# A two-layer graph kernel: the order of its opening, its scratch space, and layer 1's norms on another engine

## The chip, the cores and the metric

One core of one Trainium2 chip runs the whole program. Its engines work side by side, each through its own queue in order: TensorE (PE in the profile, with its weight loads as PEld), VectorE (DVE), ScalarE (ACT), GpSimd (POOL), and SyncE (SP), which only issues DMAs. ScalarE and GpSimd issue DMAs too. The metric is device time in microseconds; a comparison takes the median of several runs. Beside these runs one execution is recorded by the hardware profiler, and all readings of the trace are of that one.

## What is computed

The input is `x`, 2708 nodes by 256 features, and a weighted adjacency matrix `adj` of 2708 by 2708. Two layers follow each other, each inside a residual and a layer norm without weights:

```python
# layer 0: two steps of walk and attention
R = (adj + I) / row sums
for n in range(2):
    A  = top-p attention of Xa          # softmax of q k^T, smallest set of mass 0.9, normalised
    Xf = R @ Xf
    Xa = A @ Xa
    Z  = Z + Xf @ U1[n].T + Xa @ U2[n].T
h = layernorm(X + Z) * ln_g + ln_b
x = layernorm(x + h)
# layer 1: graph attention, 4 heads of 64
Wh = x @ W                              # per head
e  = leaky_relu(s_i + s_j)              # masked by adj != 0 or the diagonal
h' = softmax_j(e) @ Wh
out = layernorm(x + h')
```

So each row passes two norms at the end of layer 0 and one at the end of layer 1. ln_g and ln_b are loaded and applied as inputs.

## The kernel before, in words

Rows are cut into 22 tiles, sixteen of 128 rows and six of 110 (`rows`, `off`); `groups` are up to four tiles of the same height. Everything is float32. The loops are unrolled, and a scheduler orders the instructions of each engine, except inside `tc.manual_schedule`, where TensorE, VectorE, ScalarE and GpSimd keep the order in which the code is written. SP's queue is always ordered by the scheduler, so a load can be pulled far ahead if its buffer is free. Tiles of closed pools give their space to later pools; a new tile waits until what lay there before has been read.

**Opening** (L533 to L1072, outside the manual order). ScalarE's queue issues g_sb and b_sb (L116, L117), then the attention weights w1, w2, w3 (L539 to L542) and u_sb (L547); SP's issues x (`load_x`). Two small products make the query weights (L592 to L599). Then for each group of tiles x is transposed on TensorE (L1063), copied out by ScalarE and VectorE (L1068, L1069), and projected to q and k (`project`, L613), whose halves VectorE and ScalarE copy (L617, L618).

**Layer 0** is driven by `slot`: each call moves the searches for the top-p threshold (`going`, mostly VectorE), the rows under way (`doing`) and a stream of walk products (`walks`, L878) one step on. `walks` loads the adjacency in half columns (`blk`, pool `adjp` of 3 buffers), one block ahead. `step` runs the attention of 22 rows (`turned`, `weigh`, L225 to L243). `finish` ends a row: it adds up the terms, and for rows 0 to 17 goes through `norms` (norm, times ln_g, plus x and ln_b, norm) and `sources` (transpose, product with the layer-1 weights, exponentials, four scaled copies, store of the values to DRAM as `vd`). The four last rows are late: their sums stay in `xe` and their norms and sources run in layer 1.

**A norm** (`layernorm`, L131 to L139) is three VectorE instructions for mean and variance, a power on GpSimd for 1/sqrt, and after a `yield` one VectorE instruction that subtracts and multiplies. A `yield` gives way until the next call, so what stands behind it comes later in every queue.

**Layer 1** (`layer1`) goes through three groups of target rows (8, 8 and 6 tiles: 1024, 1024 and 660 columns), and for each through all 22 source tiles in pairs. A source tile needs its adjacency block, made 0 or 1 by ScalarE (`neighbours`, Sign and Square, L1187 and L1188), four weight tiles by VectorE (`weights`, L1258), and sixteen values and denominators products on TensorE (`values` L1269, `denominators` L1279). Masks are made three tiles ahead (`mask`), weights two. `beside` is called twice a pair and moves other work one step on: in group 0 the late rows (`prepared`) and the check of the shortcuts (`verdict`), two of them at a time (`late[:2]`); in groups 1 and 2 the rows of the group before (`settle`: transposes L1199, reciprocal L1202, `res` on ScalarE L1213, add on GpSimd L1218, norm, store on ScalarE's queue L1226). The six rows of the last group settle in a tail after the last product, with the store on SP (L1223).

The pools of layer 1 are opened in the order pp, pj (weight tiles), keep1 (the values `v` of 22 tiles, read back from `vd` by L1246), rp; `v` is laid out from the first tile used to the last.

Of the kernel before, what the change touches and what calls it, by code (L numbers as in the profile page):

```python
# [44 lines left out]
def kernel(  # L45
# [70 lines left out]
    nc.scalar.dma_start(g_sb, ln_g.partition_broadcast(P))  # L116
    nc.scalar.dma_start(b_sb, ln_b.partition_broadcast(P))  # L117
# [10 lines left out]
    def layernorm(dst, src, m):  # L128
# [12 lines left out]
        )  # L141

# [367 lines left out]
    def fast_layer0(ep, adjp):  # L510
# [77 lines left out]


        tr = ps_tr.tile([P, 4, P], F32, name="tr")  # L590
        for c in range(DC):
            nc.tensor.transpose(tr[:DA, c, :], w1_raw[:, c, :], ident)  # L592
        nc.vector.tensor_copy(w1_sb, tr[:DA, 0:DC, :])
        for c in range(DC):
            tr = ps_tr.tile([P, 4, P], F32, name="tr")
            nc.tensor.matmul(
                tr[:, 0, :DA], w1_sb[:, c, :], w2_sb, start=True, stop=True
            )
            nc.vector.tensor_copy(wkqk[:, c, 1], tr[:, 0, :DA])  # L599
# [236 lines left out]
        def walks():  # L836
# [152 lines left out]
        ahead = []  # L989
# [67 lines left out]
        for grp in groups:  # L1057
# [101 lines left out]
    def layer1(ep, adjp, r=None, verdict=None):  # L1159
        l1 = ExitStack()  # L1160

        pp, pj, keep, rp = (
            l1.enter_context(tc.tile_pool(name=name, bufs=bufs))
            for name, bufs in (("pp", 2), ("pj", 1), ("keep1", 1), ("rp", 1))
# [9 lines left out]
        for t in first:  # L1174
# [19 lines left out]
        def settle(g, t, val, den, u, last):  # L1194
# [10 lines left out]
            res = pp.tile([P, H, FO], F32, name="res", bufs=3)  # L1205
# [80 lines left out]
        def prepared(t):  # L1286

            yield from norms(t, x_late[:, t - NT + LATE, :])
# [136 lines left out]
```

## Time and profile before

| | us |
|---|---|
| median of 3 runs | 1600.37 (1599.63 to 1600.86) |
| the profiled execution | 1599.23 |
| its span | 1597.4 |
| TensorE busy | 1542.9 |
| VectorE busy | 1226.0 |
| ScalarE busy | 760.4 |
| GpSimd busy | 393.0 |

The stages by the trace: opening to 35.8; layer 0 to 1236; group 0 of layer 1 to 1364; group 1 to 1485; group 2 to 1572; tail to the end. The last VectorE instruction starts at 1587.04; between its end and the end of the span lie 9.95 us with the last store and the end of the program.

How to read the lines below. A line of waits has the engine and line that waited, what it waited for, the total, how often, and the longest. A line of the chain has start, length, engine, tile and line. A line of a timeline has start, length, engine, line, operation, tiles written and read, and shape; consecutive like instructions are merged, with their count. A line of windows has the stretch, its length, then busy time and count of PE, PEld, DVE, ACT and POOL, then the granted clock, the DMA share and GB/s. In the page's part 2 each digit is the busy share of a fortieth of the span in tenths.

### The profile page before, as it was taken

Reading aid. Unit: us, or ns where it says so; the run is one execution under the profiler, and the core shown is the slowest. Engines: PE = TensorE matmul, PEld = TensorE weight load, DVE = VectorE, ACT = ScalarE, POOL = GpSimd, SP = SyncE. Lnnn points to the kernel's source line nnn. Section 1 sums busy time; section 2 is a strip of 40 time slices with the busy share of each in tenths; the row PEclk is TensorE's granted clock in tenths of the full one; section 3 lists DMA queues with packets and bytes.
Section 4 is the critical chain, followed back from the end, with each engine's and each line's share of the span. In section 5 each row is a group of like instructions: output and inputs, shape, how many; then the busy total and the mean of one; then the engine's idle time right before and its main releaser. Section 6 shows DMA issues by size and latency. Waiting matters only on the chain.

```text
span 1597.4 us, 23674 instructions
## 1 busy us (share of the span) xinstructions
PE 1542.9 (97%) x8029; PEld 1039.1 (65%) x8029; DVE 1226.0 (77%) x3753; ACT 760.4 (48%) x1336; POOL 393.0 (25%) x798
## 2 busy tenths in 40 slices
PE   6999999999998999999999999999999999999994
PEld 3477777777776888787787788877777323333441
DVE  2777677767408876878778888888885989999995
ACT  2444444444335355545555566656643443444441
POOL 1310000000022222232223544545541210022122
PEclk9999999999999999999999999999999999999997
DMA  7200000000024333333333334333334434344331
GB/s 203 75 16 14 12 9 10 11 9 10 11 73 122 87 100 81 97 78 82 73 102 93 107 104 114 105 97 93 82 91 138 141 96 134 97 114 120 85 92 34
DMA packets 172493, 128.26 MB, mean 80 GB/s; under 512 B 44342, under 2 KB 161804, under 8 KB 172362
## 3 DMA queue, kind: packets, MB, share of 16 engines
q1 hardware_dynamic: 163654, 113.32, 27.0%
q0 software_dynamic: 3648, 9.26, 1.8%
q10 hardware_dynamic: 5060, 4.07, 0.8%
q8 instruction: 65, 1.06, 0.3%
q14 instruction: 66, 0.54, 0.1%
HBM read 111.78 MB, written 13.46 MB: 78 GB/s over the span
## 4 chain that ended last, share of the span: by engine, by line
PE 90%; DVE 6%; ACT 1%; issue 1%; POOL 1%; DMA 1%; ACTq 0%; POOLq 0%; DVEq 0%; SPq 0%
PE att L243 25%; PE walk L878 24%; PE acc L1269 13%; PE lg L643 7%; PE tr L225 6%; PE acc L1279 6%; PE tr L923 2%; PE tr L937 2%; DVE pt L1258 1%; PE tr L154 1%; PE lg L613 1%; DVE scr L814 1%; DVE scr L733 1%; PE tr L613 1%; DVE e L817 1%
## 5 line engine op out<-in xcount | busy, mean ns | idle before, releaser
L230 ACT COPY eT<-tr 128x512 f32<-128x512 f32 (+5 forms) x264 | 141.5, 536 | 278.4 <-PE tr L225 275.7
L668 ACT ACTIVATE junk<-e,minus,rth 128x2708 bf16<-128x2708 f32 (+1 forms) x88 | 232.9, 2646 | 34.7 <-POOL rth L700 33.9
L243 PE MATMUL att<-xm,eT 128*128 128x256 f32 (+3 forms) x968 | 230.9, 380 | 0.4 <-ACT xa L1007 0.4
L243 PE MATMUL att<-ba,eT 128*128 128x256 f32 (+3 forms) x968 | 230.7, 379 | 0.2 <-ACT eT L230 0.2
L878 PE MATMUL walk<-xe,blk 128*128 128x257 f32 (+3 forms) x968 | 225.3, 384 | 5.0 <-DVE xf L892 5.0
L878 PE MATMUL walk<-xm,blk 128*128 128x256 f32 (+3 forms) x968 | 221.9, 380 | 1.3 <-DVE xw L951 1.3
L1269 PE MATMUL acc<-pt,v 128*64 128x512 f32 (+3 forms) x1056 | 218.0, 549 | 2.9 <-DMA v<-v 2.7
L878 PEld LDWEIGHTS walk<-xe,blk 128*128 128x128 f32 (+3 forms) x968 | 178.4, 186 | 50.3 <-issue 12.2
L878 PEld LDWEIGHTS walk<-xm,blk 128*128 128x128 f32 (+3 forms) x968 | 177.8, 186 | 34.5 <-issue 3.4
L1258 DVE SCALAR_TENSOR_TENSOR pt<-e,tj,blk 128x1024 f32<-128x1024 f32 (+3 forms) x176 | 186.2, 1122 | 6.2 <-PE acc L1279 2.5
L243 PEld LDWEIGHTS att<-xm,eT 128*128 128x128 f32 (+3 forms) x968 | 169.6, 186 | 22.1 <-ACT xa L1007 0.8
L243 PEld LDWEIGHTS att<-ba,eT 128*128 128x128 f32 (+3 forms) x968 | 169.5, 186 | 21.7 <-ACT eT L230 0.5
L647 ACT ACTIVATE e<-lg 128x1024 f32<-128x1024 f32 (+1 forms) x132 | 121.1, 922 | 110.5 <-PE lg L643 106.8
L1269 PEld LDWEIGHTS acc<-pt,v 128*64 128x64 f32 (+1 forms) x1056 | 77.4, 137 | 132.9 <-issue 108.2
L748 DVE MAX8 cand<-e 128x8 f32<-128x170 f32 (+1 forms) x352 | 89.6, 323 | 90.6 <-ACT e L647 90.5
L225 PEld LDWEIGHTS tr<-ident,e 128*128 128x128 f32 (+3 forms) x968 | 115.0, 138 | 56.7 <-issue 21.0
L225 PE MATMUL tr<-ident,e 128*128 128x128 f32 (+3 forms) x968 | 147.1, 271 | 1.0 <-ACT eT L230 0.6
L137 POOL TENSOR_TENSOR ln_rs<-ln_ve,minus_half 128x1 f32<-128x1 f32 (+1 forms) x66 | 66.3, 1004 | 224.7 <-DVE ln_ve L135 174.6
L1258 DVE SCALAR_TENSOR_TENSOR pt<-r,tj,blk 128x1024 f32<-128x1024 f32 (+1 forms) x88 | 110.1, 1313 | 0.1
L1279 PE MATMUL acc<-pt,sb 128*32 128x512 f32 (+3 forms) x1056 | 106.8, 545 | 0.0
L1187 ACT ACTIVATE blk<-blk 128x1024 f32<-128x1024 f32 (+3 forms) x66 | 63.1, 957 | 91.3 <-DMA blk<-in_adjT_dram 80.6
L748 DVE MAX8 cand<-scr 128x8 f32<-128x97 f32 (+1 forms) x616 | 102.3, 244 | 0.0
(212 smaller groups left out, 1862.9 us busy)
## 6 DMA issues: line engine op xcount, KB each, us to landing
blk<-in_adjT_dram SPq DMA_DIRECT2D x32, 704.0 KB
blk<-in_adjT_dram SPq DMA_DIRECT2D x32, 512.0 KB
blk<-in_adjT_dram SPq DMA_DIRECT2D x48, 330.0 KB
blk<-in_adjT_dram SPq DMA_DIRECT2D x32, 320.0 KB
blk<-in_adjT_dram SPq DMA_DIRECT2D x12, 605.0 KB
blk<-in_adjT_dram SPq DMA_DIRECT2D x12, 440.0 KB
blk<-in_adjT_dram SPq DMA_DIRECT2D x18, 283.6 KB
c<-cs POOLq DMA_DIRECT2D x32, 128.0 KB, 2.0
```

What stands on the lines that cost most here:

```text
L137: nc.gpsimd.tensor_tensor(rs[:m], ve[:m], minus_half[:m], op=ALU.pow)
L225: nc.tensor.transpose(tr[: rows[t], q, :m], e[:m, off[t] : off[t + 1]], ident[:m, :m])
L230: copy(eT[:k, : len(grp), :m], tr[:k, : len(grp), :m])
L243: nc.tensor.matmul(acc, eT[: rows[t], q, :m], value(t), start=(t == 0), stop=(t == NT - 1),)
L643: nc.tensor.matmul(lg[:m, h, :w], qT[part, cols], kT[s][part, c0 : c0 + w], start=True, stop=True,)
L647: nc.scalar.activation(halves[:m, :, c0 : c0 + w], lg[:m, :, :w], AF.Exp, accum_out=zp[:m, n : n + 1],)
L668: nc.scalar.activation(junk[:m], e[:m], func, scale=rth, bias=minus1[:m], accum_out=acc)
L748: nc.vector.max(cand[:, n, :], src[:m, n * size : min(N, (n + 1) * size)])
L878: nc.tensor.matmul(ac[:m, :w], blk[: rows[j], j - j0, :m], cur[: rows[j], j, 0:w], start=(j == 0), stop=(j == NT - 1),)
L1258: nc.vector.scalar_tensor_tensor(pt[:k, :gw], targets[g][h // 2][:k, h % 2, :gw], tj[:k, j, h : h + 1], bar, op0=ALU.max, op1=ALU.mult,)
L1269: nc.tensor.matmul(acc[h // 2][c][q * FO : (q + 1) * FO, :w], v[j][:k, h, :], probs[n][h][:k, c0 : c0 + w], **at,)
L1279: nc.tensor.matmul(acc[2][c][h * 32 : (h + 1) * 32, :w], sb[:k, j, h : h + 1].to_broadcast([k, 32]), probs[n][h][:k, c0 : c0 + w], **at,)
```

## The change

Opening: g_sb, b_sb and u_sb are issued by SP behind x instead of ScalarE; the query weights, the transposes of x and the projections move into the manual order; the transposes of the next group are written ahead of the projection of the present one; each half of x is copied as soon as it is transposed; the projection's PSUM comes from another pool. Walks: two blocks are loaded ahead; a GpSimd memset of one column in the first four blocks and in the late rows' x makes these loads wait for GpSimd's place in the order; one `next(stream)` before the last row of the first attention step starts the first loads. `norms` of rows 0 to 17 gets one more `yield`. Layer 1: the order of pools and of `v`; `res` with 5 buffers instead of 3; a second form of the norm, `layernorm_beside`, for settled rows of groups 0 and 1 and for the late rows, which are normed into a tile `h2` first; all late rows and the verdict run together, each started one call after the other; in the tail ScalarE norms with scale and bias, and a round moves its rows from the newest to the oldest.

```diff
-    nc.scalar.dma_start(g_sb, ln_g.partition_broadcast(P))
-    nc.scalar.dma_start(b_sb, ln_b.partition_broadcast(P))
...
+    def layernorm_beside(dst, src, m):
+        col = {k: small.tile([P, 1], F32, name=f"lb_{k}")[:m] for k in ("nm", "sq", "rs", "nb")}
+        nm, sq, rs, nb = col.values()
+        nc.scalar.activation(dst, src, AF.Copy, accum_out=sq)
+        nc.gpsimd.tensor_scalar(nm, sq, -1.0 / D, None, op0=ALU.mult)
+        yield
+        nc.scalar.activation(dst, src, AF.Square, bias=nm, accum_out=sq)
+        nc.gpsimd.tensor_scalar(sq, sq, 1.0 / D, LN_EPS, op0=ALU.mult, op1=ALU.add)
+        nc.gpsimd.tensor_tensor(rs, sq, minus_half[:m], op=ALU.pow)
+        nc.gpsimd.tensor_mul(nb, nm, rs)
+        yield
+        nc.scalar.activation(dst, src, AF.Identity, scale=rs, bias=nb)
...
-    def norms(t, xt):
+    def norms(t, xt, norm=layernorm, other=None):
...
-        yield from layernorm(hh, hh, m)
-        nc.gpsimd.tensor_mul(hh, hh, g_sb[:m])
-        nc.gpsimd.tensor_add(hh, hh, xt[:m])
+        h2 = hh if other is None else other()[:m]
+        yield from norm(h2, hh, m)
+        nc.gpsimd.tensor_mul(h2, h2, g_sb[:m])
+        nc.gpsimd.tensor_add(h2, h2, xt[:m])
         yield
-        yield from layernorm(hh, hh, m)
+        yield from norm(hh, h2, m)
         yield
+        if t < NT - LATE:
+            yield
...
-                nc.scalar.dma_start(u_sb[:, k, :, s], u[s].rearrange("(c p) e -> p c e", p=P))
+                nc.sync.dma_start(u_sb[:, k, :, s], u[s].rearrange("(c p) e -> p c e", p=P))
+        nc.sync.dma_start(g_sb, ln_g.partition_broadcast(P))
+        nc.sync.dma_start(b_sb, ln_b.partition_broadcast(P))
...
+                if (s, t) < (0, 2):
+                    nc.gpsimd.memset(blk[:, :, 0:1], 0.0)
...
-            ahead = load(*queue[0])
+            blocks = [load(*queue[0]), load(*queue[1])]
+            yield
...
-                blk = ahead
-                if n + 1 < len(queue):
-                    ahead = load(*queue[n + 1])
+                blk = blocks.pop(0)
+                if n + 2 < len(queue):
+                    blocks.append(load(*queue[n + 2]))
...
                     if s and t >= NT - LATE:
                         ca = x_late[:, t - NT + LATE, :]
+                        nc.gpsimd.memset(ca[:, 0:1], 0.0)
...
+                if s == 0 and t == NT - 1:
+                    next(stream)
...
-            xT = x_turned[:, :, c0 : c0 + w]
-            nc.scalar.copy(xT[:, 0, :], tp[:, 0, :w])
-            nc.vector.tensor_copy(xT[:, 1, :], tp[:, 1, :w])
-            pj = ps_lg.tile([P, 2, CHUNK], F32, name="lg")[:, 0]
-            project(0, c0, w, pj, xT, nc.scalar.copy, nc.vector.tensor_copy)
+                copy = nc.vector.tensor_copy if c else nc.scalar.copy
+                copy(x_turned[:, c, c0 : c0 + w], tp[:, c, :w])
+            return c0, w
         with tc.manual_schedule(engines=engines):
+            query_weights()
+            ahead = turn_x(groups[0])
+            for n in range(len(groups)):
+                c0, w = ahead
+                if n + 1 < len(groups):
+                    ahead = turn_x(groups[n + 1])
+                pj = ps_tr.tile([P, 4, P], F32, name="tr").rearrange("p a b -> p (a b)")
+                project(
+                    0, c0, w, pj, x_turned[:, :, c0 : c0 + w],
+                    nc.scalar.copy, nc.vector.tensor_copy,
+                )
...
-        pp, pj, keep, rp = (
+        pp, pj, rp, keep = (
...
-            for name, bufs in (("pp", 2), ("pj", 1), ("keep1", 1), ("rp", 1))
+            for name, bufs in (("pp", 2), ("pj", 1), ("rp", 1), ("keep1", 1))
...
-        for t in first:
+        for t in reversed(first):
             v[t] = keep.tile([P, H, FO], F32, name=f"v{t}")
...
-            res = pp.tile([P, H, FO], F32, name="res", bufs=3)
+            res = pp.tile([P, H, FO], F32, name="res", bufs=5)
...
             o = pp.tile([P, D], F32, name="o")[:m]
-            yield from layernorm(o, flat, m)
             if last:
+                st = small.tile([P, 6], F32, name="ln_st")[:m]
+                mv = small.tile([P, 2], F32, name="ln_mv")[:m]
+                ve, rs, nb = (small.tile([P, 1], F32, name=f"ln_{k}")[:m] for k in ("ve", "rs", "nb"))
+                nc.vector.bn_stats(st, flat)
+                nc.vector.bn_aggr(mv, st)
+                nc.vector.tensor_scalar(ve, mv[:, 1:2], LN_EPS, None, op0=ALU.add)
+                nc.gpsimd.tensor_tensor(rs, ve, minus_half[:m], op=ALU.pow)
+                nc.gpsimd.tensor_scalar(nb, mv[:, 0:1], rs, -1.0, op0=ALU.mult, op1=ALU.mult)
+                yield
+                nc.scalar.activation(o, flat, AF.Identity, scale=rs, bias=nb)
                 nc.sync.dma_start(out[off[t] : off[t + 1], :], o)
                 return
+            yield from layernorm_beside(o, flat, m)
...
-            yield from norms(t, x_late[:, t - NT + LATE, :])
+            yield from norms(
+                t, x_late[:, t - NT + LATE, :], layernorm_beside,
+                lambda: pp.tile([P, D], F32, name="h2", bufs=4),
+            )
...
-        late = [prepared(t) for t in range(NT - LATE, NT)] if verdict else []
+        late = []
         if verdict:
-            late.append(verdict(aux))
+            late += [[k, prepared(NT - LATE + k)] for k in range(LATE)]
+            late.append([LATE, verdict(aux)])
...
-            for part in late[:2]:
-                if next(part, late) is late:
+            for part in list(late):
+                if part[0] > 0:
+                    part[0] -= 1
+                elif next(part[1], late) is late:
                     late.remove(part)
...
-            for part in list(running):
-                if next(part, running) is running:
-                    running.remove(part)
+            new = []
             if rest:
                 u = homes.pop(0).rearrange("p (h m) -> p h m", h=H) if homes else aux()
-                running.append(settle(*rest.pop(0), u, True))
-                next(running[-1])
+                new = [settle(*rest.pop(0), u, True)]
+                next(new[0])
+            running = [p for p in running[::-1] if next(p, running) is not running][::-1] + new
```

More of the change, by code (lines that the diff above doesn't have):

```diff
@@ L587, in fast_layer0, with query_weights @@
         rinv = keep.tile([P, NT], F32, name="rinv")
[L590 to L594, printed above, removed]
-            tr = ps_tr.tile([P, 4, P], F32, name="tr")
[L596 to L599, printed above, removed]
+        def query_weights():
+            tr = ps_tr.tile([P, 4, P], F32, name="tr")
+            for c in range(DC):
+                nc.tensor.transpose(tr[:DA, c, :], w1_raw[:, c, :], ident)
+            nc.vector.tensor_copy(w1_sb, tr[:DA, 0:DC, :])
+            for c in range(DC):
+                tr = ps_tr.tile([P, 4, P], F32, name="tr")
+                nc.tensor.matmul(
+                    tr[:, 0, :DA], w1_sb[:, c, :], w2_sb, start=True, stop=True
+                )
+                nc.vector.tensor_copy(wkqk[:, c, 1], tr[:, 0, :DA])
         def project(s, c0, w, pj, xT, copy_q, copy_k):
@@ L987, in slot @@
                     break
-        ahead = []
         def step(s, cur, spend):
@@ L1056, in fast_layer0, with turn_x @@
         )
-        for grp in groups:
+        def turn_x(grp):
             k = rows[grp[0]]
@@ L1066, in fast_layer0 @@
                     )
-            xT = x_turned[:, :, c0 : c0 + w]
-            nc.scalar.copy(xT[:, 0, :], tp[:, 0, :w])
-            nc.vector.tensor_copy(xT[:, 1, :], tp[:, 1, :w])
-            pj = ps_lg.tile([P, 2, CHUNK], F32, name="lg")[:, 0]
-            project(0, c0, w, pj, xT, nc.scalar.copy, nc.vector.tensor_copy)
-        with tc.manual_schedule(engines=engines):
+                copy = nc.vector.tensor_copy if c else nc.scalar.copy
+                copy(x_turned[:, c, c0 : c0 + w], tp[:, c, :w])
+            return c0, w
+        with tc.manual_schedule(engines=engines):
+            query_weights()
[9 more added lines that the diff above has]
+                )
+            ahead = []
             for n in range(10):
@@ L1286, in prepared @@
         def prepared(t):
-            yield from norms(t, x_late[:, t - NT + LATE, :])
+            yield from norms(
+                t, x_late[:, t - NT + LATE, :], layernorm_beside,
+                lambda: pp.tile([P, D], F32, name="h2", bufs=4),
+            )
             yield from sources(t, pp, aux, nc.scalar)
-        late = [prepared(t) for t in range(NT - LATE, NT)] if verdict else []
+        late = []
         if verdict:
-            late.append(verdict(aux))
+            late += [[k, prepared(NT - LATE + k)] for k in range(LATE)]
+            late.append([LATE, verdict(aux)])
         rest, running = [], []
         def beside(g, i):
-            for part in late[:2]:
-                if next(part, late) is late:
+            for part in list(late):
+                if part[0] > 0:
+                    part[0] -= 1
+                elif next(part[1], late) is late:
                     late.remove(part)
```

## The prediction, made before the changed kernel was built or run

> **What bounds the kernel now.** I read the page first, then TensorE's waits, the chain, windows for the stages of layer 1, and timelines of the opening, the last group and the end.
>
> From the page, parts 1 and 2:
>
> ```profile
> PE 1542.9 (97%) x8029; PEld 1039.1 (65%) x8029; DVE 1226.0 (77%) x3753; ACT 760.4 (48%) x1336; POOL 393.0 (25%) x798
> PE   6999999999998999999999999999999999999994
> ```
>
> TensorE is the bound. Its 54.5 us of idleness lie mostly in the first slice and the last; ScalarE is half empty. TensorE's waits (total, times, longest) name what stands ahead of it:
>
> ```profile
> PE tr L592 <- DMA xa<-in_w1T_dram: 9.8, 1, 9.8
> PE acc L1269 <- DMA v<-v: 2.7, 1, 2.7
> PE tr L148 <- DVE xe L139: 2.6, 1, 2.6
> ```
>
> Modelled ends can hide a late matmul, so the chain (start, length) gives what a pair of source tiles costs when nothing is late: 7.02+3.57 = 10.59 us in a 1024-wide group, 4.59+2.36 = 6.95 in the last, 660-wide one. It also gives the edges of the groups, and the opening's two ends.
>
> ```profile
> 1.69 8.02 DMA xa<-in_w1T_dram
> 35.77 1.98 PE lg L643 x8
> ...
> 1233.59 2.45 DMA v<-v
> 1353.49 7.02 PE acc L1269 x32
> 1360.51 3.57 PE acc L1279 x32
> 1500.81 4.59 PE acc L1269 x32
> 1505.40 2.36 PE acc L1279 x32
> ```
>
> Windows over groups 0, 1, 2 of layer 1:
>
> ```profile
> 1236.17:1364.08 127.91, 125.79 (x733) 39.89 (x735) 117.92 (x148) 50.72 (x79) 17.67 (x17) 0.99 0.44 125
> 1364.08:1485.15 121.07, 121.07 (x731) 38.09 (x733) 119.30 (x139) 53.11 (x81) 22.62 (x16) 1.00 0.39 108
> 1485.15:1571.78 86.63, 86.63 (x729) 38.84 (x729) 82.88 (x133) 37.26 (x75) 17.29 (x16) 1.00 0.30 81
> ```
>
> Eleven pairs alone are 116.5, 116.5 and 76.5 us. Transposes and products between pairs add about 5.4 (four late rows at 0.3+1.0, the shared line), 3.8 (eight settled rows at 0.47) and 3.8. So 6.0, 0.8 and 6.3 us are lost to lateness. In group 2 VectorE is why; its timeline:
>
> ```profile
> 1502.70 0.41 DVE L131 BATCH_NORM_STATS2 ln_st<-res 128x6 f32<-128x256 f32 x1
> 1503.44 0.17 DVE L1202 RECIPROCAL rden<-aux 128x4 f32<-128x4 f32 x1
> 1503.53 3.71 DVE L1258 SCALAR_TENSOR_TENSOR pt<-e,tj,blk 128x660 f32<-128x660 f32 x4
> 1507.16 0.40 DVE L139 TENSOR_SCALAR o<-res,ln_mv,ln_rs 128x256 f32<-128x256 f32 x1
> 1507.48 3.34 DVE L1258 SCALAR_TENSOR_TENSOR pt<-e,tj,blk 128x660 f32<-128x660 f32 x4
> 1510.75 0.41 DVE L131 BATCH_NORM_STATS2 ln_st<-res 128x6 f32<-128x256 f32 x1
> ```
>
> It repeats every 8.05 us without a gap, while TensorE needs 6.95+0.47 = 7.42.
>
> **What the Trainium skill says.** "ScalarE: Activation LUTs", Table sets: cheap functions such as copy and identity are in every set. The trace agrees so far: Copy, Sign, Square, Exp and Relu ran on one table load of 1.28 us, so I price no switch. "SBUF — State Buffer", Who interferes with whom: a VectorE instruction with two SBUF inputs and a GpSimd instruction that reads SBUF lock each other out. The trace agrees: the four `pt` above take 3.71 beside GpSimd's add and 3.34 alone, and GpSimd's power takes 1.21 there against 0.55 in the tail. "TensorE: Matmul & The Clock Gate", What's actually happening: after an idle window the array runs at half rate until it has been busy again. The trace shows 3.78 for the first four projection matmuls, 1.98 later, and 8.71 instead of 7.02 at 1295.22 after 1.6 us of idleness. "DMA: Bandwidth & Descriptors", Queues, rings and completion order: each DMA engine goes round the queues that have work. The 64 KB of w1T needed 8.02 us beside x, which fits.
>
> **The change, part by part** (us of the profiled execution, span 1597.4).
>
> Opening. w1T is issued third on ScalarE's queue, at 1.69; it goes first, as g_sb does now, at 0.73. The 0.25 MB of g and b ahead of it and the 1 MB of u leave its queue for SP behind x, where they are due only at the first `terms1`, about 28. At worst it still takes 8.02 (8.75), at best half (4.7); I take 7.3, 2.5 sooner. From 9.84 to 35.77 TensorE takes 25.9. Its work: weights 1.7, 44 transposes 5.7 (eight in 1.04), 2708 columns of projection at 1.75 per 512 9.3, half clock 2.9 (1.8 on the projections, 1.1 on transposes): 19.6. The other 6.3 are waits of each group for its two copies (0.59 and 0.69, one after the other). Turning the next group ahead of the projection covers these; I leave 1.5 and add 0.5, since x's transposes no longer fill the wait for the weights' copy. Saved 4.3, together 6.8 (3 to 9). What follows is TensorE-bound, so it is kept. The adjacency and late-x loads that a GpSimd memset now holds back, and blocks loaded two ahead, cost nothing: no matmul waits for `blk`, and 22 us of attention cover the first. If SP stood behind the memsets, 2 us.
>
> Layer 0, rows 0 to 17: one more slot between the norm and its transposes; the 2.6 wait goes (row 17, 1185.6 to 1188.2). VectorE idles 5 and 9 us soon after, so nothing is next: 2.5 (0 to 2.6).
>
> Into layer 1. The new pool order puts v of the first tiles at the end of the region, over what I reckon is `wk`; its scratch is last read at 1214.8, where v's loads now wait for the last attention matmul (1233.5). If space is freed tile by tile, 2.6 are gained, else nothing: 1.3.
>
> Group 0. Eight norms leave VectorE: 0.74 for the moments and 0.33 for the norm, 8.6. ScalarE gets three instructions each. None is in the trace in this shape; the page's 186 ns + 0.833 per element gives 0.40, each pointer operand 0.09, an overlap of 0.09 off, and an accumulator read takes 0.09 (the 1024-wide pair, 36.87 to 37.80 to 37.89): an estimate of 1.3 a norm, between 1.1 and 1.9 (L953's 0.51 thrice and two reads of 0.19). That lies in ScalarE's idle 77. But the rows are staggered by one call of `beside`, and calls 7 and 8, as 9 and 10, meet at TensorE between the same two pairs. Row 19 has its transposes in call 7 and its product in call 8, row 21 in 9 and 10. The product waits for the copy `xT`, which stands on ScalarE behind the previous row's seven activations and its store (1269.64 to 1271.42, 1.8): 1.9 of standing, twice, 3.9, and half clock may add 1 (0 to 3.4). So of 6.0 lost, 5.5 are lost again in another place: 0.5 gained (-3 to 4).
>
> Group 1: VectorE 119.3 of 121.1 is near its limit but TensorE sets it: 0.5 (-2 to 0.8).
>
> Group 2: VectorE's 8.05 fall to 6.98, under 7.42, so TensorE sets the pace. ScalarE: 4.25 a pair now (masks 2.98, `res` 0.9, store 0.34) plus 1.3, plus some 1.0 in which the Identity waits for GpSimd's three small operations (0.23, 0.55, 0.23 by L657 and the tail; the masks between give 1.5): 6.6 of 7.42. Of 6.3 lost, 5.6 gained (2 to 6.3).
>
> Tail. The powers start every 2.15 (1575.68 to 1586.45), because GpSimd's next add stands behind the power, and the power behind VectorE's moments. The new order puts the add first and lets ScalarE norm; GpSimd is the bound at 0.68+0.55+0.25 = 1.5 a row. Six rows from 1574.0 end at 1583.0, plus 0.3 to start, plus 0.5 for Identity: 1583.8 against 1587.45. Gained 3.6 (3 to 4.2). The 9.95 after it stay.
>
> Sum: 6.8+2.5+1.3+0.5+0.5+5.6+3.6 = 20.8. The span becomes 1576.6, that execution 1599.23-20.8 = 1578.4; the median shown lies 1.1 above it, so 1579.6.
>
> **The rivals.** (a) The opening's loads land no sooner, v waits as now, and the stalls of group 0 bring half clock each time: 20.8-2.5-1.3-3 = 14 gained, 1586.4. For it: DMA engines 63% busy in the first 10 us, nearly all with x, which stays. Against: the sooner issue. (b) ScalarE runs far enough ahead in group 0 that no product waits: 4 more gained, and v comes early: 1574.3. Against: the two calls really touch at TensorE. (c) Slower: ScalarE sets the pace of groups 1 and 2. It runs in order, so an Identity that waits for GpSimd holds the masks behind it, without which VectorE has no weights. It decides once a pair costs ScalarE more than 11.06 in group 1 or 7.42 in group 2. At 1.5 more in each of 16 pairs: 24 lost and the 6.1 of these groups not gained: 1600.4-14.7+24 = 1609.7. For it: GpSimd's operations stretch beside VectorE (1.21). Against: even three such make the Identity wait 2.1, 7.7 a pair in group 2 and 10 in group 1. (d) The gains of opening and tail are given back in layer 1: about 1600.
>
> **How the numbers follow.** The sum 0.57, (a) 0.18, (b) 0.13, (c) 0.08, (d) 0.04. The likeliest gives 1579.6; its own range is 1574.5 to 1584.5. Taking in (a) and (b): 1572.5 to 1590. About 0.2% (3.2 us) is what a measurement can tell from no change. Faster 0.88, same 0.04, slower 0.08.
>
> **What would show it.** First matmul near 7.3 and first scores near 29. No TensorE wait on v or on L148 in layer 0. In group 0, TensorE idle at two boundaries for ScalarE's `xT` copy. Group 2's pairs at 7.4, VectorE with gaps. In the tail, powers 1.5 apart. I am wrong if ScalarE's masks come late in groups 1 and 2, or if SP's order changes so that blocks arrive late in layer 0.

## The result, and the profile after

The changed kernel takes 1594.89 us, median of 7 runs (1593.14 to 1597.15), against 1600.37 of the kernel before, run beside it (7 runs, 1598.38 to 1601.95): a ratio of 0.9969, 95% interval 0.9959 to 0.9978. So 5.5 us are gained where 20.8 were forecast, and the time lies 4.9 above 1590, the upper end of the wider range. The profiled execution took 1593.14, its span is 1591.3; all readings below are of it.

The page of the changed kernel, busy times and TensorE by fortieths:

```profile
PE 1542.3 (97%) x8029; PEld 1037.7 (65%) x8029; DVE 1202.5 (76%) x3651; ACT 798.9 (50%) x1462; POOL 429.1 (27%) x884
PE   6999999999998999999999999999999999999994
```

VectorE has given 23.5 us away, ScalarE has taken 38.5 and GpSimd 36.1. Who does the work has moved as intended; TensorE's own work is the same.

TensorE's waits (total, times, longest):

```profile
PE lg L1086 <- ACT ba L1091: 6.4, 6, 1.6
...
PE tr L610 <- DMA xa<-in_w1T_dram: 4.8, 1, 4.8
PE aux L166 <- ACT xT L162: 3.8, 2, 2.1
PE acc L1313 <- DMA v<-v: 2.2, 1, 2.2
PE tr L631 <- ACT qT L636: 1.6, 2, 1.0
PE aux L160 <- ACT xe L153: 1.1, 1, 1.1
```

The wait for w1T is halved (9.8 before) and the one of L148 is gone. In their place stand four waits for ScalarE, 12.9 us together. The kernel before had 5.1 of them, all in the opening; this is the largest (waits of 0.6 us and less in layer 0 are left out in both):

```profile
PE lg L613 <- ACT ba L1068: 3.5, 4, 1.1
```

L1086 is a transpose of x in the opening, L160 and L166 are a late row's transposes and product in group 0 (L154 to L166 is `sources`).

Windows over groups 0, 1 and 2 of layer 1 (stretch, length, then busy time and count of PE, PEld, DVE, ACT, POOL, granted clock, DMA share, GB/s):

```profile
1231.49:1366.60 135.11, 129.95 (x733) 40.99 (x735) 118.94 (x122) 62.76 (x119) 40.28 (x41) 0.96 0.41 124
1366.60:1487.44 120.84, 120.84 (x731) 37.47 (x733) 112.14 (x107) 65.05 (x121) 33.44 (x40) 1.00 0.37 106
1487.44:1568.60 81.16, 81.16 (x728) 36.67 (x728) 75.94 (x101) 49.62 (x115) 25.45 (x40) 1.00 0.30 86
```

Group 2 is as forecast, group 0 is 7 us longer than before, at a mean clock of 0.96. By stage, each from the first or last matmul of its kind in the two traces:

| stage | forecast gain | gain in the traces |
|---|---|---|
| opening, to the first scores (35.70 to 34.10) | 6.8 | 1.6 |
| layer 0, to the last attention matmul | 2.5 | 2.6 |
| from there to the first value product (2.66 to 2.19) | 1.3 | 0.5 |
| group 0 (127.84 to 135.04) | 0.5 | -7.2 |
| group 1 (121.07 to 120.84) | 0.5 | 0.2 |
| group 2, to its last value product (84.41 to 79.06) | 5.6 | 5.4 |
| from there to the end (27.95 to 24.92) | 3.6 | 3.0 |
| sum | 20.8 | 6.1 |

The sum is the difference of the spans, 1597.4 less 1591.3. The forecast missed by 14.7 us, and two stages hold 12.9 of it: 5.2 in the opening and 7.7 in group 0.

The opening first. TensorE's timeline, start and length, in brackets the idle time ahead and what ended it:

```profile
4.78 0.61 PE L610 MATMUL tr<-ident,xa 128*64 128x128 f32 x2 [4.78 <-DMA xa<-in_w1T_dram]
...
20.42 0.60 PE L1086 MATMUL lg<-ident,xm 128*128 128x128 f32 x4
22.58 0.66 PE L1086 MATMUL lg<-ident,xm 128*128 128x128 f32 x4 [1.56 <-ACT ba L1091]
...
34.10 1.99 PE L661 MATMUL lg<-junk,qT 64*128 64x512 f32 x8
```

and ScalarE's in the same place:

```profile
21.34 0.58 ACT L636 COPY qT<-tr 64x512 f32<-64x512 f32 x1 [3.19 <-DVE junk L635]
21.95 0.58 ACT L1091 COPY ba<-lg 128x512 f32<-128x512 f32 x1
```

The first matmul starts 5.06 us sooner, but from there to the scores it takes 29.3 us, more than the 25.9 of before. The four transposes of a group's first half are followed by idle TensorE until ScalarE has copied that half, and this copy stands behind the q copy of the group before.

Group 0, TensorE:

```profile
1231.49 10.48 PE L1313 MATMUL acc<-pt,v 128*64 128x512 f32 x32 [2.19 <-DMA v<-v]
...
1267.86 0.41 PE L160 MATMUL aux<-ident,xe 110*128 110x110 f32 x2 [1.15 <-ACT xe L153]
...
1282.18 1.14 PE L166 MATMUL aux<-wx,xT 128*110 128x264 f32 x4 [2.05 <-ACT xT L162]
...
1283.61 8.56 PE L1313 MATMUL acc<-pt,v 110*64 110x512 f32 x32
...
1298.74 1.14 PE L166 MATMUL aux<-wx,xT 128*110 128x264 f32 x4 [1.74 <-ACT xT L162]
...
1299.93 8.78 PE L1313 MATMUL acc<-pt,v 128*64 128x512 f32 x32
```

A value pass (the 32 value products of a pair of source tiles) takes 7.09 when nothing is late. The group's work alone is 121.9 us by the prediction's count (116.5 for eleven pairs and 5.4 between them). Over that the group is 13.1 us late: 3.4 in the first pass, 1.15, 2.05 and 1.74 at three boundaries, 3.2 in the two slow passes that follow the stalls (8.56 and 8.78), 1.2 in a later one. Before it was 5.9. By the windows of these passes the mean granted clock is 0.84 in the first, 0.82 and 0.81 in the two after the stalls, and 1.00 in the later one. So about 1.7 us of the first pass (0.16 of its 10.48) are clock, and only the rest is VectorE, whose products come late there.

### The profile page after: what moved, and what is told of

The parts are those of the page before. It is cut to its first block, busy times and chain, and to the rows that moved or that the text cites. A ratio compares the mean times of both kernels' runs of the same rounds, so it can differ in the third digit from the quotient of the medians.

```text
span 1591.3 us, 23822 instructions
## 1 busy us (share of the span) xinstructions
PE 1542.3 (97%) x8029; PEld 1037.7 (65%) x8029; DVE 1202.5 (76%) x3651; ACT 798.9 (50%) x1462; POOL 429.1 (27%) x884
## 5 line engine op out<-in xcount | busy, mean ns | idle before, releaser
L686 ACT ACTIVATE junk<-e,minus,rth 128x2708 bf16<-128x2708 f32 (+1 forms) x88 | 232.8, 2646 | 36.1 <-POOL rth L718 35.2
L901 PEld LDWEIGHTS walk<-xe,blk 128*128 128x128 f32 (+3 forms) x968 | 178.5, 187 | 50.3 <-issue 12.6
L915 DVE TENSOR_TENSOR xf<-walk,xe 128x257 f32<-128x257 f32 (+1 forms) x22 | 9.4, 426 | 110.8 <-PE walk L901 110.8
```

The costliest lines, as they stand in the source:

```text
L686: nc.scalar.activation(junk[:m], e[:m], func, scale=rth, bias=minus1[:m], accum_out=acc)
L901: nc.tensor.matmul(ac[:m, :w], blk[: rows[j], j - j0, :m], cur[: rows[j], j, 0:w], start=(j == 0), stop=(j == NT - 1),)
L915: nc.vector.tensor_add(xf[:m], ac[:m, : D + 1], xe[:m, t, :])
```

## The experiments

Most are a single execution with its trace. Nine runs of the kernel before lay within 0.25% of their median (1597.35 to 1602.94 us), so each experiment is read from the stage that it touches, not from its total. All times of stages are counted as in the table above.

### The opening

Both halves turned before either is copied:

```diff
                         ident[:k, :k],
                     )
+            for c in range(DC):
                 copy = nc.vector.tensor_copy if c else nc.scalar.copy
                 copy(x_turned[:, c, c0 : c0 + w], tp[:, c, :w])
```

> Opening: both halves of a group of x are transposed before either is copied; nothing else is changed. Theory A (the second half's transposes stand behind ScalarE's copy of the first half, because both lie in one PSUM tile): the nine waits of L1086 on ScalarE (6.4 us in all) go, and the first scores start 4 to 5 us sooner after the first matmul than the changed kernel's 29.3 us, so near 29.5 instead of 34.1. Rival B (ScalarE's two copies a group are the limit in any order, since its q copy stands ahead): the waits move to the projections and the first scores stay within 1 us of 34.1. Everything behind the opening is alike.

Measured: 1584.24 us (1599.15 before), first scores at 24.92 against 34.10. Its TensorE:

```profile
4.79 0.61 PE L610 MATMUL tr<-ident,xa 128*64 128x128 f32 x2 [4.79 <-DMA xa<-in_w1T_dram]
...
7.51 3.52 PE L1086 MATMUL lg<-ident,xm 128*128 128x128 f32 x16
10.86 1.88 PE L631 MATMUL tr<-ba,wkqk 128*128 128x512 f32 x4
12.58 1.04 PE L1086 MATMUL lg<-ident,xm 128*128 128x128 f32 x8
...
24.92 1.99 PE L661 MATMUL lg<-junk,qT 64*128 64x512 f32 x8
```

The waits on these copies are gone (six, not nine), and 9.2 us with them, twice what was expected: 6.4 of them are the waits, and most of the rest slow passes that went with them (the projection of 512 columns that took 3.62 in the changed kernel takes 1.88 here). From the first matmul to the scores it is now 20.1.

Is it the data or the tile that is waited for? The order of the changed kernel, each half in a PSUM tile of its own:

```diff
-            tp = ps_lg.tile([P, 2, CHUNK], F32, name="lg")
             for c in range(DC):
+                tp = ps_lg.tile([P, 2, CHUNK], F32, name="lg")
```

> Opening: the order is the changed kernel's, but each half of a group of x gets a PSUM tile of its own. Theory A, in its form that the wait is one of the tile and not of the data: the waits of the second half's transposes on the copy of the first go as well, first scores at 29.5 to 31 instead of 34.1. Rival B: no change, 34.1. A third way: with half as many groups in flight per pool, the next group's transposes wait for this group's copies, and the gain is 1 to 3 us only.

Measured: 1586.12, first scores at 27.54. The one wait of L1086 that is left:

```profile
PE lg L1086 <- DVE ba L1091: 0.8, 1, 0.8
```

The six waits on ScalarE go here too, with nothing else in another order; one of 0.8 on VectorE's copy is left. So the wait was on the tile: the second half, which no copy reads before it is written, stood behind the reader of the first because both are one tile. It comes out better than the 29.5 to 31 expected; the 2.6 to the other order are that wait and a projection at 3.62 where the other has 1.88.

### Space at the edge of layer 1

By the sum of their tiles' sizes, 6 KB more in `pp` (two more `res`, four `h2`, 1 KB each) push the pool `pj` up onto attention's transposed exponentials `eT`. VectorE's first `pt` in the kernel before, 6.9 us ahead of the last attention matmul's end, and in the changed kernel, 0.1 behind it:

```profile
1226.65 10.12 DVE L1258 SCALAR_TENSOR_TENSOR pt<-e,tj,blk 128x1024 f32<-128x1024 f32 x8 [1.72 <-POOL xe L957]
...
1229.40 2.94 DVE L1302 SCALAR_TENSOR_TENSOR pt<-e,tj,blk 128x1024 f32<-128x1024 f32 x2 [8.67 <-PE att L258]
```

The test gives `h2` a pool of its own, opened last:

```diff
-            for name, bufs in (("pp", 2), ("pj", 1), ("rp", 1), ("keep1", 1))
+            for name, bufs in (("pp", 2), ("pj", 1), ("rp", 1), ("keep1", 1), ("hp", 4))
...
-                lambda: pp.tile([P, D], F32, name="h2", bufs=4),
+                lambda: hp.tile([P, D], F32, name="h2"),
```

> Layer 1's four h2 tiles move from the pool pp to a pool of their own, opened last, so that pt and its neighbours lie 4 KB lower. Theory A (space: 6 KB more in pp pushed pt onto attention's last tiles, and VectorE's first pt waits 8.7 us for the last attention matmul): the first pt starts 4 to 7 us before the attention's end (at 1222 to 1226 instead of 1229.4), and the first pair of group 0 takes 7.0 to 7.1 instead of 10.5, so group 0 takes 131.7 instead of 135.1. Rival B (pt waits for its inputs, the mask or the exponentials, which come late): no change, 10.5 and 135.1.

VectorE in the same place of this run, and TensorE's first pass:

```profile
1225.46 14.44 DVE L1302 SCALAR_TENSOR_TENSOR pt<-e,tj,blk 128x1024 f32<-128x1024 f32 x12 [1.86 <-POOL xe L980]
...
1234.90 8.78 PE L1313 MATMUL acc<-pt,v 128*64 128x512 f32 x32 [2.14 <-DMA v<-v]
```

VectorE starts 7.3 us ahead of the attention's end again, and group 0 takes 131.59, so 3.4 us hung on where four tiles of 1 KB lie. Only 1.7 of them are in the first pass: it is 8.78 rather than 7.0, with no wait but that on v ahead of it, a slow pass (mean clock 0.80). The wait of L160, 1.15 in the changed kernel, is gone too, and the slow pass late in the group is 0.5 shorter. The total, 1592.96, is only 0.2 below the changed kernel's profiled execution (1593.14), because three places ahead of group 0 took longer: 1.7 us in the opening, where a pass ran slow in this execution (3.10 for 1.90 after a wait of 0.9 that cost nothing in the changed kernel), 1.1 in a slow walk pass (10.13 from 516.43, where the changed kernel has 8.90), after a wait of 3.2 that both have, and 0.6 at the attention's end, half of it a wait of 0.34 on `eT`. The Trainium skill, "TensorE: Matmul & The Clock Gate", What's actually happening, says that the window in which the array's activity is judged runs freely. If so, it depends on where a wait falls whether it costs a slow pass; these two runs, within 0.1 us of each other up to the wait of 0.9, agree.

Then v. The changed order put the first tiles of v over space that is free early, yet their loads still start at the attention's end. SP issues the first of them at 1229.33, after 8.7 us of waiting for the attention matmuls. Theory: a pool waits for all that lay under its whole range. On top of the run above, ten tiles of v go into a second pool:

```diff
+            home = keep_first if t in first[:10] else keep
-            v[t] = keep.tile([P, H, FO], F32, name=f"v{t}")
+            v[t] = home.tile([P, H, FO], F32, name=f"v{t}")
```

> On top of the pool for h2: v of the first ten source tiles lies in a pool of its own, opened last, beyond what attention still reads; the other twelve stay where they were. Theory A (space waits for every tile under a pool's whole range, and the range of keep1 reaches over attention's last inputs): v's loads are issued before the last attention matmul, the wait of 2.1 to 2.2 us on v goes, group 0 starts 0 to 0.3 us after the attention's end, and its first pair runs at full clock, 10.6 instead of 12.3. Rival B (v's loads stand on SP's queue behind mask blocks that land late, or what is written last into v's source is late): the wait stays at about 2.2.

TensorE of this run:

```profile
1224.04 3.44 PE L258 MATMUL att<-ba,eT 128*110 128x256 f32 x8 [2.59 <-ACT eT L245]
...
1235.04 7.09 PE L1316 MATMUL acc<-pt,v 128*64 128x512 f32 x32 [0.56 <-ACT xa L1030]
```

and its ScalarE:

```profile
1221.43 1.06 ACT L1224 ACTIVATE blk<-blk 128x1024 f32<-128x1024 f32 x1 [5.84 <-DMA blk<-in_adjT_dram]
...
1223.48 0.94 ACT L245 COPY eT<-tr 128x440 f32<-128x440 f32 x2
```

The wait on v is gone, the first pass has full speed, and group 0 takes 128.76, as theory A says; rival B falls. That a pool waits as a whole, and not tile by tile, is not shown apart from this: the new pool differs both in being a pool of its own and in its place, and where v's first tiles lay before is reckoned from tile sizes. But the stretch from layer 0's first walk to attention's end is 3.7 us longer than in the run before: ScalarE's second mask stands ahead of an attention copy in its queue and waits for its block, beside 1.3 MB of v. The total is 1590.74.

### The late rows in group 0

How far a single execution of this group can be trusted: four kernels have the changed kernel's group 0 unaltered, and it takes 135.04 (changed), 135.29 (both halves turned), 134.71 (a tile per half) and 136.39 (settled rows on VectorE, below).

First, started two calls apart:

```diff
-            late += [[k, prepared(NT - LATE + k)] for k in range(LATE)]
-            late.append([LATE, verdict(aux)])
+            late += [[2 * k, prepared(NT - LATE + k)] for k in range(LATE)]
+            late.append([2 * LATE, verdict(aux)])
```

> The late rows start two calls apart instead of one, and the verdict follows after eight calls instead of four; nothing else is changed. Theory A (the prediction's: a row's product meets the previous row's transposes at one boundary, and its xT copy stands behind that row's ScalarE work): the two stalls at about 1282 and 1299 (2.05 and 1.74 us) go, and with them the two slow passes after them (8.5 and 8.7 instead of 7.05 each half), so group 0 takes 128 instead of 135.1. Rival B (ScalarE waits on GpSimd's small operations at each norm, wherever it is started): the stalls stay or come one by one at more boundaries, group 0 at 133 to 136. Rival C: the rows end later, the last of them and the verdict reach into the late part of group 0 and cost there what is gained, 133 to 136.

Measured: 1596.6, group 0 at 138.09, longer than the 135.04 of the changed kernel. The two waits of L166 are gone, but three of L160 take their place, 6.8 us together. ScalarE at one of them:

```profile
1281.41 0.17 ACT L170 ACTIVATE sb<-aux 110x4 f32<-110x4 f32 x1 [2.27 <-PE aux L166]
...
1282.58 0.57 ACTq L179 DMA_DIRECT2D v<-cs  x1
1283.19 0.60 ACT L153 ACTIVATE xe<-h,lb_nb,lb_rs 110x256 f32<-110x256 f32 x1 [0.65 <-POOL h L188]
```

The Identity (L153) of one row stands behind seven activations and a store that read the previous row's product, and TensorE wants that row's transposes at this same boundary. Two calls of `beside` meet at every boundary, so a stagger in calls only chooses which two steps collide. My theory A was right on the stalls it named and wrong on the cure; rival B had the form right, waits one by one at other boundaries, though here the Identity waits in ScalarE's queue and not for GpSimd. This run shows one thing more: GpSimd and VectorE at its start,

```profile
1242.03 12.89 POOL L149 TENSOR_SCALAR lb_sq<-lb_sq 110x1 f32<-110x1 f32 x1 [7.39 <-ACT h L148]
```

```profile
1229.94 24.94 DVE L1302 SCALAR_TENSOR_TENSOR pt<-e,tj,blk 128x1024 f32<-128x1024 f32 x20 [8.70 <-PE att L258]
```

An operation on one column, 0.2 us when alone, ends only when VectorE's unbroken row of products ends, at 1254.9. An Identity of ScalarE waited 9.31 us on the chain behind it, the next mask stood behind that Identity, and the third pass took 9.21 instead of 7.09. So about 2 of the 3 us by which this group is longer than the changed kernel's come from there.

Next, the late rows normed by VectorE as before, still one call apart (`layernorm` in place of `layernorm_beside` in `prepared`):

> The late rows are normed by VectorE again, into h2 as in the changed kernel and one call apart. A norm takes one call fewer, so a row's transposes come two calls sooner. Theory A (what stalls group 0 is where the transposes and products of a row meet at TensorE): the two stalls of L166 on xT, 1.7 to 2.1 each, stay in the one form or the other, while the wait of L160 (1.15) goes; group 0 at 133 to 135. Rival B (ScalarE's norms with GpSimd's small operations are the cause): all three stalls go and group 0 falls to about 129.5 or below, 3.4 of lateness at its start left in it. Theory C: with VectorE starting late and 8.6 us of norms back on it, the masks' products come late, and group 0 takes over 136.

```profile
PE aux L166 <- ACT xT L162: 3.8, 2, 2.0
...
PE aux L160 <- DVE xe L137: 2.1, 1, 2.1
```

Group 0 takes 137.32. Both stalls of L166 stay at their length, so they don't come from ScalarE's norms; the wait of L160 changes its engine. With VectorE starting late, its norms cost 2.3 us more than ScalarE's in this execution, not much more than the scatter of this group. A is right on the two stalls and wrong on the third wait, C on the number, and B falls. The total, 1592.68, is no measure of it: see the end of this document.

Then the steps placed by boundary: a row's transposes first at one, its product at a later one, a whole pair between, two PSUM tiles at most at a boundary:

```diff
+            k = t - NT + LATE
+            for _ in range((1, 0, 3, 4)[k]):
+                yield
+            part = sources(t, pp, aux, nc.scalar)
+            next(part)
+            yield
+            yield
+            yield from part
-            yield from sources(t, pp, aux, nc.scalar)
...
-            late.append([LATE, verdict(aux)])
+            late.append([LATE + 7, verdict(aux)])
```

> The late rows keep their start, one call apart, and their norms on ScalarE; only their transposes and products are moved: a row's transposes stand at the start of a boundary between two pairs, its product a whole pair after them, at most two of them at a boundary, and the verdict starts seven calls later. Theory A (a step that TensorE takes at the same boundary as the ScalarE work that it needs is what stalls, and each stall brings a slow pass after it; the norms themselves keep up): the waits of L160 and L166 on ScalarE go (4.95 us in the changed kernel), so do the two slow passes (3.2), and group 0 takes 126.5 to 128 instead of 135.1. Rival B (GpSimd's small operations beside VectorE hold the norms up by more than the room given): stalls of 1 to 2.5 us stay at one or more boundaries, group 0 at 130 to 134. Rival C: the later products push the masks on ScalarE, and the stall comes back as late masks in the second half of group 0.

Measured: 1590.58, no wait of L160 or L166 left, but group 0 at 131.8 and not 128: TensorE now waits twice for `pt` itself in the third pair (1.1), and the first pass and those of pairs 3 to 5 are long at a granted clock of 1.00. VectorE's start is still late in this run: it stands idle for 9.7 us until the last attention matmul, and the first pass takes 10.37. For the third pair the trace has the chain:

```profile
1242.19 12.82 POOL L149 TENSOR_SCALAR lb_sq<-lb_sq 110x1 f32<-110x1 f32 x1 [7.46 <-ACT h L148]
...
1255.97 0.60 ACT L153 ACTIVATE h<-xe,lb_nb,lb_rs 110x256 f32<-110x256 f32 x1 [8.26 <-POOL lb_nb L151]
...
1259.53 10.61 DVE L1302 SCALAR_TENSOR_TENSOR pt<-e,tj,blk 128x1024 f32<-128x1024 f32 x8 [4.57 <-ACT blk L1222]
...
1260.87 3.94 PE L1313 MATMUL acc<-pt,v 128*64 128x512 f32 x10 [0.53 <-DVE pt L1302]
```

GpSimd's one-column operation is held up to the end of VectorE's row again, ScalarE's Identity waits for it, the mask waits behind the Identity, VectorE waits for the mask, and the third pair takes 3.6 us longer than the second. That is rival B, with its 130 to 134, though the stall comes at the products and not at a boundary. It is not this edit's doing: the run with the settled rows on VectorE has the same hold-up (12.82) and the same third pair.

### The settled rows

The norm of groups 0 and 1 back on VectorE (`layernorm` in place of `layernorm_beside` in `settle`):

> The settled rows of groups 0 and 1 are normed by VectorE again, as in the kernel before; the late rows and all else stay as changed. Theory A (VectorE sets the pace of group 2 before, and ScalarE's norms of settled rows are what frees it): group 2 from first to last value product takes 84.4 instead of 79.06, group 1 stays at 120.8, group 0 at 135. Rival B (group 2's gain comes from the changed homes and from five res tiles): group 2 stays at 79.1.

Measured: 1598.73; group 2 takes 84.41, to the hundredth that of the kernel before, group 1 121.07, group 0, which this edit leaves alone, 136.39. VectorE in group 2, this run and then the changed kernel:

```profile
1508.48 3.71 DVE L1302 SCALAR_TENSOR_TENSOR pt<-e,tj,blk 128x660 f32<-128x660 f32 x4
1512.11 0.40 DVE L137 TENSOR_SCALAR o<-res,ln_mv,ln_rs 128x256 f32<-128x256 f32 x1
1512.43 3.34 DVE L1302 SCALAR_TENSOR_TENSOR pt<-e,tj,blk 128x660 f32<-128x660 f32 x4
```

```profile
1505.09 3.32 DVE L1302 SCALAR_TENSOR_TENSOR pt<-e,tj,blk 128x660 f32<-128x660 f32 x4
1509.01 3.74 DVE L1302 SCALAR_TENSOR_TENSOR pt<-e,tj,blk 128x660 f32<-128x660 f32 x4 [0.60 <-ACT blk L1221]
```

Without the norms VectorE has room and waits for its mask; with them it has none. Group 2's gain is the norms' alone.

### Put together

The opening's order, `hp`, and a second pool for only the first four tiles of v:

> Together: the opening with both halves turned before either is copied, h2 in a pool of its own, and v in two pools, but with only the first four source tiles of v in the early one (0.5 MB ahead of attention's end, not 1.3). Theory A (the late attention copy with ten early v's came from their 1.3 MB, which held back the mask block on whose mask ScalarE then waited): the wait of L258 on eT, 2.6, goes, v's wait goes too, first scores near 25, attention ends near 1220, group 0 starts 0 to 0.6 behind it and takes 128 to 129; the run is at 1576 to 1579 against 1594.9 of the changed kernel. Rival B (any early v disturbs attention's end): the wait on eT stays at 1 to 3 us, and the run is at 1579 to 1582.

Measured: 1577.5; group 0 starts 0.6 after attention's end and takes 127.23, but 1.9 of the wait on `eT` stay (theory A on the total, rival B on that point). With the late rows by boundary as well:

> The same with the late rows' transposes and products a pair apart as well. Theory A (the stalls of group 0 were where the rows meet at TensorE; what was left with that edit alone, VectorE's products late in pairs 3 to 5, came from the late start of VectorE): group 0 takes 122 to 125, the run is at 1570 to 1575, 1.6 to 1.9% faster than the kernel before. Rival B (VectorE or the masks are late in the middle of group 0 wherever they start): group 0 at 127 to 129, and the run no better than 1576.

Measured: 1573.07, median of 5 (1570.86 to 1574.22), against 1600.28 of before (9 runs): a ratio of 0.9834, interval 0.982 to 0.9847. The traced execution is the fastest of the five. Its window of group 0:

```profile
1221.97:1344.43 122.46, 122.46 (x731) 38.99 (x732) 112.44 (x117) 62.92 (x117) 41.59 (x41) 1.00 0.43 129
```

TensorE is busy through all of it at full clock; 122.46 is within 0.6 of the 121.9 of its work. What the edit by boundary left when alone (131.8) is gone here, where VectorE starts early, v lies ready and no one-column operation of GpSimd takes more than 1.5 us in this group; which of the three gave how much is not separated. Against the changed kernel's trace the 22.3 us of shorter span are 9.8 in the opening, 1.6 in the start of group 0 and 12.6 in it, less 1.9 at attention's end, and 0.2 after group 2.

Last, two early tiles of v, and each mask's block issued ahead of its v:

> As the last version, with only the first two source tiles of v in the early pool (0.25 MB) and, at each mask, the block issued before the tile of v. Theory A (the early v's bytes hold back the second mask block, on whose mask ScalarE waits with attention's copy behind it: 0.3 us of waiting on eT with no early v, 1.9 with four tiles, 2.6 with ten): the wait of L258 on eT falls to 0.3 to 1.2, group 0 starts 0.6 behind attention's end as before, and the run gains 0.5 to 1.5 us on 1573. Rival B (the wait comes from the start of the mask's products elsewhere): the wait stays at 1.9, the run at 1573.

Measured: 1572.89 (5 runs, 1572.79 to 1573.35; ratio 0.9834, 0.9819 to 0.9849): no faster. The longest wait on `eT` is 1.4, and group 0 takes 124.04. Over 0, 2, 4 and 10 early tiles the wait is 0.3, 1.4, 1.9 and 2.6, so it grows with them, yet two already bring most of it. The row is not a clean one: the run with two tiles also issues in another order, and the run by boundary has 0.7 with no early tile at all. That bytes are a part of the cause fits; it is not shown, and the rest stays open.

## Why the prediction was wrong

It fails in two steps.

**Opening**, 6.8 forecast, 1.6 measured. The step that failed is "Turning the next group ahead of the projection covers these; I leave 1.5": it was to save 4.3 us, and the stretch from first matmul to scores grew by 3.5 instead. The diff's other half, each half copied as soon as it is turned, I priced at nothing; it put a wait for ScalarE between the halves, 6.4 us, with slow passes after them. The rest of that step was right in mechanism: with the copies after both halves, TensorE needs 20.1 from first matmul to scores, where the step's own sum is 19.6+1.5+0.5 = 21.6. The term ahead of it was too small: w1T's first place in its queue is worth 5.06, not 2.5; w1T landed at what the step called the best case, and with the 2.5 alone the opening would have come out slower than before.

**Group 0**, 0.5 forecast, -7.2 measured. The two stalls are where the prediction put them and of its size (2.05 and 1.74 for 1.9 twice). Its sum has a slip there: 3.9 and 1 make 4.9, not the 5.5 that it takes off. What failed is what it added to the stalls. Half clock, put at 1, cost 3.2 in the two passes behind them, and about 1.7 in the first pass, behind the wait on v, where it was put at nothing. And space was put at nothing: I looked at the new order of pools for v alone and did not ask what the two more `res` and four `h2` push up. The pool run gives 3.4 of that back: 1.7 in the first pass, 1.15 at the wait for row 18's Identity, 0.5 in a later pass. Row 18's Identity hangs on GpSimd's chain, three small operations counted at 1.0 us together, which take 3.0 there beside VectorE's products (from 1264.21 on in the trace: 1.08, 1.53 and 0.19 with their gaps). In the pool run they take 2.7 (from 1257.18 on), but there the Identity is done 6.0 us before TensorE comes: the late start and the stretch make this wait together. I had named the stretch of the power, 1.21 for 0.55, but used it only in the rival for groups 1 and 2, not in group 0, where VectorE has no gaps.

**Into layer 1**, 1.3, the middle of an open question, measured 0.5. Reversing the tiles within the pool did not free v's loads: they still waited for the last attention matmul. The wait of 2.2 went only with a pool apart, which fits space that comes free by pool and does not prove it.

**Tail**, 3.6, measured 3.0. The powers start about every 1.5 us as worked out (1572.49, 1573.96, 1575.52, 1577.07); the Identity is 0.60 instead of 0.5, and the rest is at its two ends.

Right, and for the reasons given: layer 0 (2.6 for 2.5), group 1 (0.2 for 0.5), group 2 (5.4 for 5.6, by VectorE falling below TensorE's 7.42; the pairs come every 7.42). ScalarE's norm, 0.40+0.19, 0.49+0.19 and 0.60 with overlaps, takes 1.4 from start to start (from 1276.59 on in the trace), close to the estimated 1.3; the price was that of the Trainium skill, "ScalarE: Activation LUTs", What ACT_TABLE_LOAD costs. Rival (c) did not come about in groups 1 and 2. But its chain, an Identity that waits for GpSimd with the masks behind it, is what stopped group 0 in three of the test kernels. Rival (a) erred with the sum: it too kept the opening's 4.3. Of (d), that layer 1 gives gains back, group 0's part came true.

## What to carry to other kernels

A wait is not covered by work written ahead of it if the new order puts a reader of the same tile between two of its writers: follow each tile's writers and readers in the new order, whole tiles and not halves. When a change adds tiles to a pool, work out the address of every pool opened after it, and ask what each now lies on and when that was last read. Where two hooks meet between the same two stretches of TensorE work, place steps by boundary, so that a whole stretch lies between a step and the engine work that it needs.

## What was not expected of the hardware

GpSimd's operation of one column that took 12.89 us is longer than one product of VectorE (24.94/20 = 1.25 us) by a factor of ten. It is no single case: the same operation took 12.82 in two other kernels (settled rows on VectorE, steps by boundary), and one addition of 110x256 took 5.6 to 7.1 in three (the pool for `h2`, ten and two early tiles of v) where it takes 0.73 alone. Each of the six ended within 0.7 us of the end of VectorE's unbroken row. The Trainium skill, "SBUF — State Buffer", Who interferes with whom, says that a VectorE instruction with two SBUF inputs contends with a GpSimd instruction that reads SBUF, and of VectorE's two-port modes that whoever issues first has the shared ports for the whole instruction. Here GpSimd was kept out over several instructions in a row, up to ten, while in the changed kernel, beside a longer row (31.65 us), such operations came in after about one each (0.7 to 1.5). What decides between the two I can't tell from these runs.

The end of the program is GpSimd's: one drain of it takes 6.7 us in every trace. Between its last branch and that drain lie 2.9 to 3.4 us in eleven kernels, and 0.5 in the two with norms put back on VectorE (late rows, settled rows), whose totals are so 2.4 us better than their stages. No edit touched that place; the cause was not looked for.
